# Two mixtures of experts inside a scan kernel: every expert over every token, or each token sorted to its two experts

## The chip, the cores and the metric

The kernel runs on one core of one Trainium2 chip. A core has five engines with queues of their own, each in order: TensorE (PE; its weight loads are listed as PEld), VectorE (DVE), ScalarE (ACT), GpSimd (POOL) and SyncE (SP), which here issues nearly all DMAs. [...] The metric is the device time of one execution in microseconds. Three runs of the kernel before gave 7050.43, 7048.9 and 7061.08 us, with the median 7050.43.

## The reference, cut to what matters

The model has four layers on an input of 4 images of 32 x 32 positions with 256 channels, that is 4 images of 1024 tokens. Layer 0 is a state-space block (512 inner channels, 64 states), layer 1 a convolution block, layer 2 graph attention and a mixture of experts, layer 3 a second state-space block (512 inner channels, 16 states) and a second mixture. The mixtures are the matter here:

```python
# layer 2                                          # layer 3
logits = tokens @ router_w.T                       logits = xf @ gate_w + gate_b
probs = softmax(logits)                            probs = softmax(logits)
rw, re = top_k(probs, 2)                           top2_vals, top2_idx = top_k(probs, 2)
rw = rw / max(rw.sum(-1), 1e-12)
combine = zeros(N, 8).at[rows, re].set(rw)         cw = zeros(N, 8).at[rows, top2_idx].add(top2_vals)
out = tokens
for e in range(8):                                 for each expert:
    h = gelu(tokens @ w1[e] + b1[e])                   h = gelu(xf @ w1 + bb1)
    y = h @ w2[e] + b2[e]                              y = h @ w2 + bb2
    out = out + combine[:, e:e+1] * y                  acc = acc + we[:, None] * y
```

Tokens are the layer-normed activations, and both results are added to the residual. The hidden width is 256 in layer 2 and 512 in layer 3. The weight of six of a token's eight experts is zero, so a token needs two experts only; the reference computes all eight. Everything is f32.

## The kernel before, in words

The work goes image by image. `SCANS` lists eight scans: four of layer 0, named (0, image), and four of layer 3, named (3, image), in the order (0,0) (0,1) (3,0) (0,2) (3,1) (0,3) (3,2) (3,3). A scan is cut into units of 128 partitions by 1024 time steps: 256 units for a layer-0 scan and 64 for a layer-3 scan, 1280 in all. A unit k (function `scans`, line 340 on) does this:

- SP loads the row or rows of step sizes into `dA`, spread over the partitions: two DMAs per unit for layer 0, eight for layer 3. There are five buffers, and the load is written four units ahead.
- ScalarE takes their exponential. PE spreads the inputs into PSUM (`ps_rep`).
- VectorE multiplies `ps_rep` with the row of B and runs the scan itself into `h` (five buffers). POOL multiplies `h` with the row of C.
- PE sums pairs of units over the states into `ps_y`.

All other work is "stages" (`STAGES`): `front` (layer 0 up to the scan), `middle` of an image (the rest of layer 0, layer 1, attention, the layer-2 mixture `moe(2, ...)`, and the front of layer 3) and `last` (the back of layer 3 and `moe(3, ...)`). A stage is a Python generator. `run` (line 503) drives the scans; after every half unit it calls `advance` up to two times, and each call writes down a small piece of the current stage, up to its next `yield`. It stops as long as an estimate of some engine's time, kept by `Metered`, is ahead of VectorE's. So the order of instructions in every engine's queue is fixed when the program is built: pieces of a stage stand between scan units. A stage waits for the scan that it is listed with. Where a scan needs a stage that isn't finished, `need` (line 478) writes the rest of that stage at once, with no scan beside it. After the last unit the rest of the stages is written out, and `last` of image 3 runs alone.

In this order, `middle` of images 0, 1 and 2 and `last` of images 0 and 1 stand wholly under scans. `middle` of image 3 stands partly under scan (3,2) and for its larger part alone, because scan (3,3) needs it. `last` of image 2 stands under scan (3,3) with its second half behind the last unit, and `last` of image 3 stands alone at the end.

`moe` (line 1347) normalizes the tokens into `xn`, transposes them into `xT` (two chunks of 128 channels by 1024 tokens), multiplies with the router into `lg`, and `route` turns that into `cw`, a weight for each token and expert, zero for all but two. The term with b2 is one matmul with `cw` transposed. Then it goes over 16 blocks, each one expert and 512 tokens. PE multiplies with `we1` into `ps_h` (line 298), ScalarE takes the gelu into `h_m` (line 1441), PE multiplies with `we2` into `ps_e` (line 1433), and VectorE adds `ps_e` times the token's weight to the residual `tb` (line 1449). Each expert's weights are loaded once per image, by SP (lines 1350 and 1352), with two buffers. PSUM for the stages is three banks taken in turn (`ps`).

In the profile, instructions recorded through `Metered` all bear line 120; the names of tiles tell them apart.

Of the kernel before, what the change touches and what calls it, by code (L numbers as in the profile page):

```python
# [16 lines left out]
P = 128  # L17
NB = 4
L = 1024
# [5 lines left out]
NEXP = 8  # L25
NEG = -1.0e30
# [29 lines left out]
    (("L2_ffn_b1", 16), ("L3_ffn_b1", 32)),  # L56
# [31 lines left out]
class Metered:  # L88
# [21 lines left out]
    def __getattr__(self, key):  # L110
        got = getattr(self.what, key)
        if self.name is None:
            return Metered(got, self.clock, key) if key in self.COST else got
        cost = self.COST[self.name].get(key)
        if cost is None:
            return got

        def run(*args, **kw):
            self.clock[self.name] += cost(*args, **kw)
            return got(*args, **kw)  # L120

        return run


class Hybrid:
# [352 lines left out]
    def need(self, scan):  # L478

        late = False  # L480
        while ("parts", *scan, DC - 1) not in self.ready:
            if self.advance() is None:
# [6 lines left out]
    def advance(self):  # L489

        if self.stage is None:
# [6 lines left out]
        if cost is None:  # L498
            self.stage = None
            return 0.0  # L500
        return cost

    def run(self):

        self.done, self.ready = set(), set()
        self.todo, self.stage = list(STAGES), None
# [6 lines left out]
        with tc.tile_pool(name="scan", bufs=1) as mp, tc.tile_pool(  # L513
# [6 lines left out]
            for n, _ in enumerate(self.scans(mp, psum)):  # L520
# [3 lines left out]
                for e in clock:  # L524
                    clock[e] = max(clock[e], now - LAG)
                for _ in range(TICKS):
                    if max(clock.values()) > clock["vector"] + LEAD or self.advance() is None:
                        break
            while self.advance() is not None:
# [778 lines left out]
    def prepare_moe(self, st, psum):  # L1308
# [22 lines left out]
        self.gb = self.const.tile([P, NEXP], F32, name="gb")  # L1331
# [4 lines left out]
    def moe(self, which, b, tb):  # L1336

        nc, tc, a = self.nc, self.tc, self.a
        w1, w2, b1, hidden = (
            (a["L2_ffn_w1"], a["L2_ffn_w2"], self.vec["L2_ffn_b1"], 256) if which == 2  # L1340
            else (a["L3_ffn_W1"], a["L3_ffn_W2"], self.vec["L3_ffn_b1"], 512)
        )
        KH = hidden // P
        with tc.tile_pool(name=f"m{which}{b}", bufs=1, side="right") as op:
            xT = op.tile([P, 2, L], F32, name="xTm")
            cw = op.tile([P, TB, NEXP], F32, name="cw")

            def expert_weights(e):
                we1 = op.tile([P, 2, hidden], F32, tag="we1", name="we1", bufs=2)
                nc.sync.dma_start(we1, w1[e].rearrange("(k p) n -> p k n", p=P))  # L1350
                we2 = op.tile([P, KH, C], F32, tag="we2", name="we2", bufs=2)
                nc.sync.dma_start(we2, w2[e].rearrange("(k p) n -> p k n", p=P))
                return we1, we2

            weights = {0: expert_weights(0)}
            with tc.tile_pool(name=f"mg{which}{b}", bufs=1, side="right") as gp:
                xn = gp.tile([P, TB, C], F32, name="xnm")
                yield from self.norm(gp, tb, TB, xn, "lnm")
                yield from self.turned(xn, TB, xT)
# [16 lines left out]
                if which == 2:  # L1376
                    for j in range(0, TB, 2):
                        tj = tb[:, j : j + 2, :]
                        nc.gpsimd.tensor_tensor(tj, tj, xn[:, j : j + 2, :], ALU.add)
                        yield 0.6  # L1380
                yield from self.route(gp, lg, cw, which == 2)
# [12 lines left out]
                got = {}  # L1394
# [15 lines left out]

            hidden_of = {}
            got = {}

            def one(item):
                kind, e, g, i = item
                we1, we2 = weights[e]
                if kind == "h":
                    if i == 0:
                        hidden_of[e, g] = op.tile([P, KH, 512], F32, tag="h", name="h_m", bufs=2)
                        if g == 1 and e + 1 < NEXP:  # L1420
                            weights[e + 1] = expert_weights(e + 1)
                    got[item] = ps = self.ps("ps_h")
                    self.mm(
                        ps, lambda k: we1[:, k, i * P : (i + 1) * P], xT, 2,
                        slice(g * 512, (g + 1) * 512),
                    )
                    return
                h = hidden_of[e, g]
                got[item] = ps = self.ps("ps_e", (P, 2, C))
                for s in range(2):  # L1430
                    m = 2 * i + s
                    for f in range(KH):
                        nc.tensor.matmul(  # L1433
                            ps[:, s, :], lhsT=h[:, f, m * P : (m + 1) * P], rhs=we2[:, f, :],
                            start=(f == 0), stop=(f == KH - 1),
                        )

            def two(item):
                kind, e, g, i = item
                if kind == "h":  # L1440
                    nc.scalar.activation(
                        hidden_of[e, g][:, i, :], got.pop(item), AF.Gelu,
                        bias=b1[:, e * KH + i : e * KH + i + 1],
                    )
                    return
                ps = got.pop(item)
                for s in range(2):
                    m = 4 * g + 2 * i + s
                    nc.vector.scalar_tensor_tensor(  # L1449
                        tb[:, m, :], ps[:, s, :], cw[:, m, e : e + 1], tb[:, m, :],  # L1450
                        ALU.mult, ALU.add,
# [3 lines left out]
            blocks = [(e, g) for e in range(NEXP) for g in range(2)]  # L1455
            for n in range(len(blocks) + 1):
                if n < len(blocks):
# [272 lines left out]
```

## Time and profile before

| What | us |
|---|---|
| median of three runs | 7050.43 |
| the profiled execution | 7061.6 |
| its span, first to last instruction | 7059.5 |
| PE busy in it | 5383.6 |
| VectorE busy in it | 5212.0 |
| POOL busy in it | 3650.0 |
| ScalarE busy in it | 3462.1 |
| VectorE's scan instructions, 1280 | 2924.7 |
| VectorE's products ahead of them, 1280 | 1553.0 |
| POOL's products behind them, 1280 | 3024.2 |

The first scan instruction starts 317.7 us into the span and the last ends at about 6643. From 5743 to 6280 no scan runs, while `middle` of image 3 is finished. The last mixture's experts run from 6830.7 to 7053.1.

A line of the groups by line reads: line, engine, operation, output<-inputs by the program's names, shapes, count | busy us, mean ns of one | idle time of the engine just before them, and what ended it. The DMA share is the busy share of the core's 16 DMA engines.

### The profile page before, as it was taken

Reading aid. Unit: us, or ns where it says so; the run is one execution under the profiler, and the core shown is the slowest. Engines: PE = TensorE matmul, PEld = TensorE weight load, DVE = VectorE, ACT = ScalarE, POOL = GpSimd, SP = SyncE. Lnnn points to the kernel's source line nnn. Section 1 sums busy time; section 2 is a strip of 40 time slices with the busy share of each in tenths; the row PEclk is TensorE's granted clock in tenths of the full one; section 3 lists DMA queues with packets and bytes.
Section 4 is the critical chain, followed back from the end, with each engine's and each line's share of the span. In section 5 each row is a group of like instructions: output and inputs, shape, how many; then the busy total and the mean of one; then the engine's idle time right before and its main releaser. Section 6 shows DMA issues by size and latency. Waiting matters only on the chain. (4 is left out here: it accounts for less than half of the span.)

```text
span 7059.5 us, 66331 instructions
## 1 busy us (share of the span) xinstructions
PE 5383.6 (76%) x20516; PEld 2218.2 (31%) x20516; DVE 5212.0 (74%) x4477; ACT 3462.1 (49%) x4162; POOL 3650.0 (52%) x1801
## 2 busy tenths in 40 slices
PE   7185876578898567879779668898698677957979
PEld 3020221032253022224235332242254322513556
DVE  2787898887898986789889877898899831247511
ACT  3254666244477324447658434577386332244511
POOL 1288677664556754555766554556656520045300
PEclk9585876578888567979879778898698889877989
DMA  2355666654456565446656654456666620135421
GB/s 82 77 139 158 161 178 167 169 143 120 115 143 176 160 172 136 119 116 171 176 151 164 178 144 120 115 143 178 165 168 165 162 70 6 44 107 152 113 63 33
DMA packets 395053, 939.03 MB, mean 133 GB/s; under 512 B 83268, under 2 KB 165776, under 8 KB 393040
## 3 DMA queue, kind: packets, MB, share of 16 engines
q1 hardware_dynamic: 392512, 932.10, 49.0%
q8 instruction: 172, 2.82, 0.2%
q0 software_dynamic: 2128, 2.13, 0.2%
q14 instruction: 241, 1.97, 0.1%
HBM read 844.17 MB, written 93.95 MB: 133 GB/s over the span
## 5 line engine op out<-in xcount | busy, mean ns | idle before, releaser
L120 POOL TENSOR_TENSOR h<-h,rows 128x1024 f32<-128x1024 f32 x1280 | 3024.2, 2365 | 2138.8 <-DVE h L120 1756.0
L120 DVE TENSOR_TENSOR_SCAN h<-dA,ps_rep 128x1024 f32<-128x1024 f32 x1280 | 2924.7, 2285 | 228.0 <-issue 94.6
L120 DVE TENSOR_TENSOR ps_rep<-ps_rep,rows 128x1024 f32<-128x1024 f32 x1280 | 1553.0, 1213 | 338.7 <-PE ps_rep L120 317.0
L120 ACT ACTIVATE dA<-dA,A_L_conv_A_log 128x1024 f32<-128x1024 f32 x1024 | 1152.8, 1145 | 695.2 <-DMA dA<-dt 600.6
L120 PE MATMUL ps_rep<-S,spread_L_conv_A_log 96*128 96x512 bf16 x2048 | 763.2, 463 | 899.6 <-DVE h L120 731.7
L120 PE MATMUL ps_y<-h,collect_L_conv_A_log 128*32 128x512 f32 x4096 | 750.2, 755 | 91.1 <-POOL h L120 91.1
L120 ACT ACT_TABLE_LOAD x494 | 633.8, 1283 | 174.7 <-DMA dA<-dt 115.0
L120 PEld LDWEIGHTS <-spread_L_conv_A_log 96*128 96x128 bf16 x2048 | 164.5, 103 | 1661.3 <-DVE h L120 1213.5
L120 PE MATMUL ps_h<-xTm,we 128*128 128x512 f32 x1280 | 605.2, 609 | 7.6 <-ACT h_m L120 6.6
L120 PE MATMUL ps_e<-we,h_m 128*128 128x256 f32 x2560 | 587.9, 381 | 10.1 <-ACT h_m L120 10.1
L120 ACT ACTIVATE p<-ps_sc 128x512 f32<-128x512 f32 x512 | 277.9, 595 | 587.2 <-PE ps_sc L120 573.8
L120 ACT ACTIVATE dA<-dA,A_L_attn_A_log 128x1024 f32<-128x1024 f32 x256 | 293.6, 1148 | 490.1 <-DMA dA<-dt 456.4
L120 PEld LDWEIGHTS ps_e<-we,h_m 128*128 128x128 f32 x2560 | 481.8, 190 | 140.6 <-issue 46.0
L120 PE MATMUL ps_at<-p,v 128*32 128x512 f32 x1024 | 363.6, 627 | 63.1 <-ACT p L120 55.7
L120 PE MATMUL ps_rep<-S,spread_L_attn_A_log 96*128 96x512 bf16 x512 | 191.4, 464 | 280.8 <-DVE h L120 239.2
L120 ACT ACTIVATE h_m<-ps_h,cols 128x512 f32<-128x512 f32 x320 | 216.5, 687 | 302.2 <-PE ps_h L120 299.3
L120 DVE SCALAR_TENSOR_TENSOR tb<-ps_e,cw,tb 128x256 f32<-128x256 f32 x448 | 192.6, 473 | 200.5 <-PE ps_e L120 200.5
L120 PEld LDWEIGHTS ps_h<-xTm,we 128*128 128x128 f32 x1280 | 242.4, 193 | 288.1 <-issue 236.3
L120 PE MATMUL ps_sc<-qT,kT 32*128 32x512 f32 x1024 | 300.7, 663 | 0.0
L120 PE MATMUL ps_at<-p,ones 128*32 128x512 f32 x1024 | 280.1, 627 | 0.0
L120 DVE RECIPROCAL sums<-sums 128x512 f32<-128x512 f32 x16 | 53.6, 3353 | 253.4 <-ACT sums L120 253.4
L120 PEld LDWEIGHTS ps_y<-h,collect_L_conv_A_log 128*32 128x32 f32 x4096 | 98.8, 119 | 450.4 <-issue 234.3
(406 smaller groups left out, 5703.5 us busy)
## 6 DMA issues: line engine op xcount, KB each, us to landing
dA<-dt SPq DMA_DIRECT2D x2048, 256.0 KB
dA<-dt SPq DMA_DIRECT2D x2048, 64.0 KB
we<-in_L_ffn_W_dram SPq DMA_DIRECT2D x64, 512.0 KB
parts<-parts SPq DMA_DIRECT2D x64, 384.0 KB
S<-parts SPq DMA_DIRECT2D x96, 256.0 KB
dt<-sp_r SPq DMA_DIRECT2D x64, 256.0 KB
y<-yo SPq DMA_DIRECT2D x128, 128.0 KB
y_back<-y SPq DMA_DIRECT2D x64, 256.0 KB
```

What stands on the lines that cost most here:

```text
L120: return got(*args, **kw)
```

## The change

Each token now goes to its two experts only. The 2048 pairs of token and expert of an image are put in order by expert, each expert's run is rounded up to whole tiles of 256, and 15 tiles are computed whatever the routing (2048 / 256 + 8 - 1 is the most that rounding can ask for). In detail:

- `xn` is stored to DRAM as rows (`rows`), one row of 1 KB per token.
- `route` keeps the two choices apart (`hot`), and the new `sort` works out, with small matmuls and comparisons: how many tokens each expert has, how many tiles that makes, the place of each pair in the order (`place`), the expert of each tile (`expert`), the token of each place (`token`), each pair's weight (`share`), and the b1 column of each tile (`bias`).
- For each tile, SP reads the expert's number into a register and loads that expert's weights from the address it gives (again for every tile, four and five buffers, two tiles ahead). POOL gathers the tile's 256 rows with two indirect DMAs of 128 rows. PE transposes them, and then runs the two matmuls with the gelu between as before, on 256 rows. ScalarE copies the result out of PSUM, and SP stores it in DRAM (`done`).
- At the end, POOL gathers each token's two results with 16 indirect DMAs (`y_b`, four buffers), and VectorE adds them times `share` to `tb`, one tile two steps after its gather.
- `Hold` is a `yield` that keeps stages from advancing for some half units of the scan, unless they are forced: `advance` compares the half unit with `until`.
- The addition of `xn` to the layer-2 residual moves behind the b2 term; the b1 vectors move out of the packed vectors into tiles of their own; `prepare_moe` makes a few constant tables.

The diff, cut to its core:

```diff
+SLOTS = 256
+TILES = 2 * L // SLOTS + NEXP - 1
...
-    def advance(self):
-
+    def advance(self, forced=False):
+
+        if self.half < self.until and not forced:
+            return None
...
+        if isinstance(cost, Hold):
+            self.until = self.half + cost
...
-            xT = op.tile([P, 2, L], F32, name="xTm")
-            cw = op.tile([P, TB, NEXP], F32, name="cw")
-
-            def expert_weights(e):
-                we1 = op.tile([P, 2, hidden], F32, tag="we1", name="we1", bufs=2)
-                nc.sync.dma_start(we1, w1[e].rearrange("(k p) n -> p k n", p=P))
-                we2 = op.tile([P, KH, C], F32, tag="we2", name="we2", bufs=2)
-                nc.sync.dma_start(we2, w2[e].rearrange("(k p) n -> p k n", p=P))
-                return we1, we2
...
+            def room(n):
+                xs[n] = [op.tile([P, C], F32, tag=f"x{s}", name=f"x_t{s}", bufs=3) for s in range(NS)]
+
+            def gather(n, s):
+                if n < TILES:
+                    x = xs[n][s]
+                    nc.gpsimd.indirect_dma_start(
+                        out=x, out_offset=None, in_=rows,
+                        in_offset=bass.IndirectOffsetOnAxis(
+                            ap=token[:, NS * n + s : NS * n + s + 1], axis=0
+                        ),
+                        bounds_check=L - 1, oob_is_err=False,
+                    )
...
+            def weights(n):
+                if n < TILES:
+                    e = nc.sync.value_load(expert[:, n : n + 1], min_val=0, max_val=NEXP - 1)
+                    for w, to in zip((w1, w2), we[n]):
+                        nc.sync.dma_start(to, w[bass.ds(e, 1)].rearrange("o p k n -> (o p) k n"))
...
+                nc.sync.dma_start(rows.rearrange("(p j) c -> p j c", j=TB), xn)
...
-                yield from self.route(gp, lg, cw, which == 2)
+                yield from self.route(gp, lg, cw, hot, both, which == 2)
+                yield from self.sort(gp, which, hot, both, cw, place, share, token, expert, bias)
+                for n in range(2):
+                    weights(n)
+                    gather(n, 0)
+                    gather(n, 1)
+                    yield 1.0
+                gather(2, 1)
...
+                if kind == "x":
+                    if n + 2 < TILES:
+                        weight_room(n + 2)
+                    weights(n + 2)
+                    ps = got[item] = self.ps("ps_xt", (P, 2, NS, P))
+                    for k in range(2):
+                        for s in range(NS):
+                            nc.tensor.transpose(
+                                ps[:, k, s, :], xs[n][s][:, k * P : (k + 1) * P], self.ident
+                            )
...
+                    gather(n + 2, 0)
...
+                    yo = op.tile([P, NS, C], F32, tag="yt", name="y_t", bufs=2)
+                    nc.scalar.copy(yo, got.pop(("o", n)))
+                    nc.sync.dma_start(
+                        done[n * SLOTS : (n + 1) * SLOTS, :].rearrange("(s p) c -> p s c", p=P), yo
                     )
...
-                for s in range(2):
-                    m = 4 * g + 2 * i + s
-                    nc.vector.scalar_tensor_tensor(
-                        tb[:, m, :], ps[:, s, :], cw[:, m, e : e + 1], tb[:, m, :],
-                        ALU.mult, ALU.add,
-                    )
...
+            yield from self.pipe(items, one, two, cost=1.7)
+            yield Hold(4)
+
+            def back(q):
+                y = got[q] = op.tile([P, C], F32, tag="yb", name="y_b", bufs=4)
+                nc.gpsimd.indirect_dma_start(
+                    out=y, out_offset=None, in_=done,
+                    in_offset=bass.IndirectOffsetOnAxis(ap=place[:, q : q + 1], axis=0),
+                    bounds_check=TILES * SLOTS - 1, oob_is_err=False,
+                )
...
+            def add(q):
+                i, j = divmod(q, TB)
+                nc.vector.scalar_tensor_tensor(
+                    tb[:, j, :], got.pop(q), share[:, i, j : j + 1], tb[:, j, :],
+                    ALU.mult, ALU.add,
+                )
+
+            yield from self.pipe(range(2 * TB), back, wait, add, cost=1.0)
+
+    def sort(self, gp, which, hot, both, cw, place, share, token, expert, bias):
...
+        nc.vector.tensor_tensor(
+            reach, placef.unsqueeze(2).to_broadcast([P, 2 * TB, blocks + 1]),
+            self.block.unsqueeze(1).to_broadcast([P, 2 * TB, blocks + 1]), ALU.is_ge,
+        )
...
+        at = gp.tile([P, 2 * TB, P], BF16, name="at")
+        nc.vector.tensor_tensor(
+            at, low.unsqueeze(2).to_broadcast([P, 2 * TB, P]),
+            self.count.unsqueeze(1).to_broadcast([P, 2 * TB, P]), ALU.is_equal,
+        )
+        yield 2.2
+
+        own = gp.tile([P, 2 * TB, blocks], F32, name="own")
+        nc.gpsimd.tensor_tensor(own, reach[:, :, :blocks], reach[:, :, 1:], ALU.subtract)
+        of = gp.tile([P, 2, 2 * TB, blocks], BF16, name="of")
+        nc.vector.tensor_scalar(of[:, 0], own, self.part8, None, ALU.mult)
+        nc.gpsimd.tensor_tensor(
+            of[:, 1].rearrange("p (i j) k -> p i j k", i=2),
+            own.rearrange("p (i j) k -> p i j k", i=2),
+            self.count[:, :TB].unsqueeze(1).unsqueeze(3).to_broadcast([P, 2, TB, blocks]), ALU.mult,
+        )
+        yield Hold(2)
+        ps = self.ps("ps_tk")
+        for q in range(2 * TB):
+            for i in range(2):
+                nc.tensor.matmul(
+                    ps[:, :blocks], lhsT=at[:, q, :], rhs=of[:, i, q, :],
+                    start=(q == 0 and i == 0), stop=(q == 2 * TB - 1 and i == 1),
+                )
...
+        nc.vector.tensor_copy(token, ps[:, :blocks])
```

## The prediction

> **What bounds the kernel now.** I read the page first, then the busy times by stretch, the chain of waits, the groups by line and SP's own waits. The page says that no engine is busy throughout, so the bound has to be read stage by stage.
>
> ```profile
> span 7059.5 us, 66331 instructions
> PE 5383.6 (76%) x20516; PEld 2218.2 (31%) x20516; DVE 5212.0 (74%) x4477; ACT 3462.1 (49%) x4162; POOL 3650.0 (52%) x1801
> L120 DVE TENSOR_TENSOR_SCAN h<-dA,ps_rep 128x1024 f32<-128x1024 f32 x1280 | 2924.7, 2285 | 228.0 <-issue 94.6
> L120 DVE TENSOR_TENSOR ps_rep<-ps_rep,rows 128x1024 f32<-128x1024 f32 x1280 | 1553.0, 1213 | 338.7 <-PE ps_rep L120 317.0
> L120 DVE SCALAR_TENSOR_TENSOR tb<-ps_e,cw,tb 128x256 f32<-128x256 f32 x448 | 192.6, 473 | 200.5 <-PE ps_e L120 200.5
> ```
>
> A scan unit costs VectorE 2.285 + 1.213 = 3.50 us, and 1280 of them are 4478 us of the span. The other stages are threaded between the units, except where no scan can run. By stretch:
>
> ```profile
> 3670.60:3961.90 291.30, 280.91 (x1168) 151.26 (x1166) 278.96 (x213) 237.07 (x223) 176.32 (x75) 1.00 0.61 164
> 4634.00:4770.80 136.80, 133.57 (x551) 73.61 (x549) 132.64 (x130) 115.35 (x108) 75.49 (x32) 1.00 0.57 149
> 5743.00:6279.60 536.60, 435.51 (x1612) 185.89 (x1611) 82.96 (x189) 180.21 (x298) 61.98 (x50) 0.91 0.09 31
> 6499.00:6641.00 142.00, 126.52 (x506) 66.37 (x504) 122.94 (x92) 107.06 (x103) 76.24 (x33) 0.98 0.58 151
> 6641.00:6758.00 117.00, 115.38 (x421) 77.20 (x420) 17.64 (x37) 22.80 (x33) 3.82 (x2) 1.00 0.10 30
> 6831.00:7053.00 222.00, 222.00 (x768) 146.16 (x767) 27.63 (x63) 43.97 (x64) 0.00 (x0) 0.99 0.09 29
> ```
>
> The columns are stretch, length, then PE, PEld, VectorE, ScalarE and POOL busy, PE clock, DMA share, GB/s. Rows one and two are the experts of a layer-3 and a layer-2 mixture under a scan: VectorE is 96% busy, so a unit waits for VectorE. Row three has one layer-2 mixture (6031 to 6144) without a scan, rows five and six are layer-3 mixtures after the last scan: PE alone. The chain shows one block of 512 tokens and one expert there, 6.87 + 6.91 = 13.78 us, 16 of them 220 us:
>
> ```profile
> 7004.84 6.87 PE ps_h L298 x16
> 7011.71 6.91 PE ps_e L1433 x32
> ```
>
> In row four the scan is (3,3) with eight row loads a unit. SP waited there almost only for a DMA's semaphore, never long for a free buffer, so SP's issue sets the pace:
>
> ```profile
> SPq L394 <- DMA we<-in_L_ffn_W_dram: 6.1, 4, 2.4
> SPq L394 <- DVE h L120: 0.7, 2, 0.4
> ```
>
> **What the Trainium skill says.** "SBUF — State Buffer", Who interferes with whom: a VectorE instruction with two SBUF inputs contends with a GpSimd instruction that reads SBUF. The trace agrees: the split's subtraction takes 691 ns when free and 1546 in the median, beside POOL's 2.37 us products. Sums read from PSUM (the 473 ns row) show no such spread.
>
> ```profile
> L120 DVE TENSOR_TENSOR sp_x<-sp_l,parts x56: 691/1546/2171, 532.5 to 6277.5; 128x512 f32<-128x512 f32 x56
> L120 POOL DMA_INDIRECT mask_dram<-zero,where x64: 993/1001/1316, 322.7 to 599.2; - x64
> ```
>
> "DMA: Bandwidth & Descriptors", SWDGE vs HWDGE vs iDMA: DMAs of POOL and of SP end on the same 16 engines, which take turns between queues. No run here has both heavy. The same page, Latency and other measured facts, puts a load of a register from memory at some 600 ns; the attention's own on SP shows 281 ns and 0.6 us with the checks behind it.
>
> **The change, part by part.**
>
> *PE work.* Before, each layer-3 mixture is 16 x 13.78 = 220 us and each layer-2 one 110 (half the hidden width; its 113 us agree). After, a 256-row tile is half a block, 6.9 us (3.45 in layer 2), plus four transposes of 0.31 us (16 took 5.03 us at 6804.7) = 1.26. So 15 x 8.18 = 123 us and 15 x 4.70 = 71 us. Less 97 and 39.
>
> *Added chain.* The sort is some 20 small VectorE steps (0.17 to 0.28 each, like the router's), three long ones (496 elements 0.65, 464 elements 0.65, 2048 elements 2.4, scaled from 1.2 ns an element), two POOL products of 480 elements (1.2 each), 32 small matmuls (estimate 3.5): about 15 us on end. The bias term behind it (9 us, 6822 to 6831) hides the first gathers (1.0 us on POOL, 2.1 to 3.2 us to landing) and first weights. At the end come the last store (ScalarE copy 0.6, SP 0.45, landing about 2.2), 16 gathers back at 1.0 us each on POOL and one landing and sum (4): 23.5 us.
>
> *Where PE is alone.* Last mixture: from 6821.8 comes 15 + 9 + 2 (fill) + 123 + 23.5 = end at 6994, against 7053.6: **-59 us**. Mixture of row five: before, 113 us remain after the last scan. In the changed program's order 3 tiles' transposes, 4 tiles' first and 5.5 tiles' second matmuls stand behind the last unit: 3 x 1.26 + 9.5 x 3.45 = 37, plus 23.5 = 60: **-53**. Layer-2 mixture of row three: 6022 + 15 + 9 + 71 + 23.5 = 6141 against 6144: **0** (within 12).
>
> *SP in row four.* Per tile a register load with checks 0.6, two loads at a computed address 2 x 0.55, a store 0.5 = 2.2 us. 11 tiles fall under scan (3,3): 24, less 2.8 for the loads of before: **+22**, since every row load of the scan is queued behind on SP. Under the other scans (two loads a unit, 1.1 us of 3.5) SP has room.
>
> *Under the scans: six mixtures.* VectorE loses 64 x 0.473 = 30.3 us and some 4 us of waits for the first expert. It gains the sort, 8 us, the 16 sums, 16 x 0.475 = 7.6, and waits: the first of a run of two-SBUF-input steps behind POOL's product waits 0.7 to 2.0 us (five to eight of them, 8 us); the sort's steps wait for PE twice (1.7 each, as the router's first copy does) and for POOL's product (2.6); the sums come two ticks behind their gather, less than 1.0 + 3.2 us, about 4. Sum 34.5 against 34.5: **0**. POOL: 46 x 1.01 + 2.4 = 49 us more a mixture; in 69 units its products are 163 us, so 212 of some 265: it fits. Behind a POOL wait stand the scan's products, five buffers deep.
>
> *DMA under the scans.* Row six moves 6.4 MB (222 us at 29 GB/s) in 20 us of 16-engine time: 3.1 us/MB. Row one is 178 us of it for 76 units; less 26 for 8.4 MB of weights, 2.0 us a unit. A layer-3 tile is now 1.05 MB of weights, 0.26 gathered, 0.26 stored, 4.9 us per 3.4 units: 1.44. Together **3.44 of 3.50 us**. Layer 2: 3.25 per 2.2 units, 1.48: 3.5. The row loads run four units ahead, so I let a unit stretch by 0.2 us over 33 or 51 units: **+8** a mixture, +48. Bounds: 0 (the share reached 1.0 in short bursts) to +25, if the queues reach 85% only (4.1 us a unit).
>
> Sum: -59 - 53 + 22 + 48 = **-42**. Against the profiled span of 7059.5 us (2.1 us less than that execution's time, 7061.6) that is 7017.5; on the median, 7050.4, it is **7008 us**.
>
> **Rivals.**
> - *DMA becomes the bound under the scans* (other side). Place: the gather phases of the six mixtures; price 0.6 us a unit, 25 us a mixture, 102 more than above: 7110. It decides from 15 to 16 us a mixture (unit 3.86 us), where the 90 us saved without scans are spent. For it: 3.44 of 3.5 us demanded, and weights stand before row loads in SP's one queue. Against: VectorE ran 3.5 us a unit at share 0.65 (2338 to 2555).
> - *VectorE's 30 us come free*: sums and sort cost 15.5 us without waits and DMA is hidden, -19 a mixture: -114 - 90, about 6850 to 6900. Against: the 1546 ns row.
> - *Gathering costs POOL twice as much* (2 us for rows of 1 KB; the trace has only 4-byte elements): POOL then needs 260 of 265 us a mixture, units wait for their product buffers, and each tail of gathers grows by 16: +30 a mixture, +48 in the tails: about 7230.
> - That it doesn't do what it says is excluded by the program's order: 15 tiles of transposes and matmuls stand in each mixture.
>
> **How the numbers follow.** Chances: forecast 0.45 (own range 6955 to 7045), DMA rival 0.35, free VectorE 0.12, dear gathers 0.08. 0.2% is 14 us, about what a measurement of this kernel can tell from no change. Of the forecast 0.38 lies below 7036 and 0.07 within; of the DMA rival 0.02 is within. Faster 0.38 + 0.12 = 0.50, same 0.09, slower 0.41. The range cuts half of the free case and the dear one: 6910 to 7150.
>
> **What would show it.** Right: the last mixture near 170 us with PE at 8.2 us a tile; the stretch after the last scan down by half; the layer-2 mixture without a scan unchanged; scan (3,3) longer by 20 us with SP without gaps; under scans, about the same time for the same units, DMA share above 0.85. Wrong: ScalarE waiting for row loads by tens of us a mixture (DMA), POOL above 90% (gathers), VectorE idle before sums or the token list (the waits are longer than I set), or a tile without a scan above 8.2 us because weights or rows come late.

## The result, and the profile after

The changed kernel takes 7138.55 us in the median of four runs (7117.31 to 7146.82), where the kernel before took 7050.0 beside it: a ratio of 1.0117, interval 1.0093 to 1.0142. So it is 1.2% slower. In a later comparison the ratio was 1.0119 (1.0102 to 1.0136). The forecast was 7008; its own range ended at 7045, the range over all its cases at 7150.

The engines are less busy than before, PE by 468 us, and the span is longer. These are lines of the page of the changed kernel: the span, the busy times and three groups (busy and mean, then idle time before and what ended it).

```profile
span 7115.6 us, 67338 instructions
PE 4915.4 (69%) x19731; PEld 1998.0 (28%) x19731; DVE 5193.8 (73%) x4260; ACT 3266.2 (46%) x4222; POOL 4048.1 (57%) x2186
L123 ACT ACTIVATE dA<-dA,A_L_conv_A_log 128x1024 f32<-128x1024 f32 x1024 | 1158.5, 1146 | 968.0 <-DMA dA<-dt 880.9
L123 POOL DMA_INDIRECT x_t<-rows,token x210 | 215.3, 1025 | 58.2 <-issue 31.7
L123 DVE SCALAR_TENSOR_TENSOR tb<-y_b,share,tb 128x256 f32<-128x256 f32 x112 | 89.0, 813 | 182.2 <-DMA y_b<-done,place 182.2
```

The same group of exponentials, in the page of the kernel before:

```profile
L120 ACT ACTIVATE dA<-dA,A_L_conv_A_log 128x1024 f32<-128x1024 f32 x1024 | 1152.8, 1145 | 695.2 <-DMA dA<-dt 600.6
```

ScalarE waits 280 us longer for the scan's row loads. Of VectorE's 182 us for gathered rows, 137 stand where no scan runs, in stages where it waited 184 us for `ps_e` before; under the scans it is 45 us, where 17 for `ps_e` stood. A sum that took 473 ns takes 813 in the mean: 484 without a scan, 922 to 975 in the five mixtures under scans. A gather of 128 rows costs POOL 1.03 us, as forecast. Now by stretch (stretch, length, busy PE, PEld, VectorE, ScalarE, POOL, PE clock, DMA share, GB/s): the tiles of a layer-3 and of a layer-2 mixture under a scan, layer 2 of image 3 alone, scan (3,3), the rest of layer 3 of image 2, the last mixture's tiles and its gathers back.

```profile
3756.40:3956.90 200.50, 171.59 (x838) 111.04 (x836) 171.82 (x101) 162.32 (x195) 143.18 (x76) 0.96 0.92 238
4733.00:4871.00 138.00, 103.62 (x502) 61.28 (x501) 115.14 (x70) 104.25 (x125) 113.21 (x67) 0.91 0.91 235
5888.00:6414.70 526.70, 388.39 (x1584) 168.09 (x1583) 70.52 (x161) 187.39 (x327) 112.54 (x98) 0.87 0.19 59
6640.20:6820.80 180.60, 133.97 (x580) 87.88 (x581) 114.06 (x67) 112.91 (x137) 100.29 (x55) 0.86 0.82 201
6823.00:6895.00 72.00, 33.88 (x159) 27.74 (x157) 7.82 (x17) 11.43 (x25) 20.19 (x20) 0.75 0.38 116
6969.00:7082.00 113.00, 112.53 (x535) 98.56 (x535) 0.00 (x0) 41.55 (x89) 23.09 (x23) 0.97 0.58 164
7082.00:7110.00 28.00, 0.18 (x1) 0.00 (x0) 7.68 (x16) 0.58 (x1) 16.28 (x16) 0.55 0.28 85
```

Row one is where VectorE was 96% busy; it is 86% busy now, and the DMA engines are at 0.92. Where PE is alone the change does what it says: 113 us for 15 tiles. The chain of the tail shows a tile, 3.46 + 3.45 us and 0.44 of transposes, and the drain behind the last one:

```profile
7020.84 3.46 PE ps_h L1522 x16
7024.29 3.45 PE ps_e L1530 x16
...
7082.26 0.59 ACT y_t L1551
7082.87 2.12 DMA done<-y_t
7085.99 5.49 DMA y_b<-done,place x2
```

The starts of the scan instructions in the two traces give the account by stretch (a number of a unit is the number of its scan instruction). Up to unit 1203 the scans took 5425.5 us and take 5575.9 (+150); layer 2 of image 3, alone between units 1203 and 1204, 536.4 and 526.5 (-10); units 1204 to 1279, with scan (3,3), 361.7 and 406.1 (+44); what follows, 418.2 and 294.8 (-123). The second profile of the changed kernel, 7130.1 us long and nearer its median, has 5592.8, 526.3, 404.9 and 293.1; the comparisons below are with that one. The tails came about as forecast (-112 and 0). The scans cost 195 to 210 us, where +70 was forecast (48 for the DMAs, 22 for SP). The experiments ask what these are. PE's granted clock fell too, from 1.00 to 0.96 in row one, but PE is busy 171.6 of 200.5 us there; whether a lower clock adds to the loss was not tried by itself.

One suspect was not in the forecast. SP's own waits among the tiles of row one (total us, times, longest):

```profile
SPq L1552 <- ACT y_t L123: 81.5, 14, 8.0
SPq L401 <- DVE h L123: 11.0, 14, 2.3
SPq L401 <- DMA we<-in_L_ffn_W_dram: 8.4, 5, 3.5
```

Line 1552 is the store of a finished tile. SP stands 81.5 of 200.5 us at it, waiting for ScalarE's copy, with the row loads (line 401) queued behind. So beside "the bytes fill the DMA engines" (D) there is "SP's one queue is held up" (Q).

How a late row load reaches VectorE is read from three waits of the same stretch together:

```profile
ACT dA L123 <- DMA dA<-dt: 27.6, 10, 8.8
PE ps_h L123 <- ACT y_t L123: 19.2, 10, 2.9
DVE ps_rep L123 <- PE ps_rep L123: 15.2, 11, 4.4
```

ScalarE waits for the row at its exponential, with a tile's copy `y_t` behind it; PE waits for that copy to free a bank, with the scan's `ps_rep` behind; and VectorE waits for `ps_rep`.

### The profile page after: what moved, and what is told of

It is laid out like the page before. It is cut to its first block, busy times and chain, and to the rows that moved or that the text cites. A ratio compares the mean times of both kernels' runs of the same rounds, so it can differ in the third digit from the quotient of the medians.

```text
span 7115.6 us, 67338 instructions
## 1 busy us (share of the span) xinstructions
PE 4915.4 (69%) x19731; PEld 1998.0 (28%) x19731; DVE 5193.8 (73%) x4260; ACT 3266.2 (46%) x4222; POOL 4048.1 (57%) x2186
## 5 line engine op out<-in xcount | busy, mean ns | idle before, releaser
L123 PE MATMUL ps_rep<-S,spread_L_conv_A_log 96*128 96x512 bf16 x2048 | 794.7, 480 | 1152.0 <-DVE h L123 962.7
L123 PE MATMUL ps_y<-h,collect_L_conv_A_log 128*32 128x512 f32 x4096 | 802.0, 793 | 88.9 <-POOL h L123 88.7
L123 PE MATMUL ps_h<-x_tt,we 128*128 128x256 f32 x1200 | 330.3, 425 | 126.9 <-ACT y_t L123 77.0
L123 PE MATMUL ps_e<-we,h_m 128*128 128x256 f32 x1200 | 294.8, 387 | 11.2 <-ACT y_t L123 6.5
L123 PEld LDWEIGHTS ps_h<-x_tt,we 128*128 128x128 f32 x1200 | 241.6, 209 | 214.2 <-ACT y_t L123 94.3
L123 PEld LDWEIGHTS ps_e<-we,h_m 128*128 128x128 f32 x1200 | 228.2, 193 | 83.8 <-issue 24.4
L123 POOL DMA_INDIRECT x_t<-rows,token x210 | 215.3, 1025 | 58.2 <-issue 31.7
L123 DVE SCALAR_TENSOR_TENSOR tb<-y_b,share,tb 128x256 f32<-128x256 f32 x112 | 89.0, 813 | 182.2 <-DMA y_b<-done,place 182.2
```

## The experiments

Ratios are to the kernel before on the same chip; 0.001 is 7 us. Four comparisons gave the kernel before 7049, 7057, 7046 and 7051 us, so ratios are compared, and a gain against the changed kernel is the difference of two ratios. Each ratio has an interval of 8 to 17 us to either side; medians of one comparison differ from such a gain by up to 7 us.

**Sorted only where no scan runs.** The dense mixture of before is kept beside the new one, and each mixture picks one:

```diff
+SORTED = [(2, 3), (3, 3)]
     def moe(self, which, b, tb):
+        if (which, b) in SORTED:
+            yield from self.moe_sorted(which, b, tb)
+        else:
+            yield from self.moe_dense(which, b, tb)
```

> The sorted form only where no scan runs beside it: layer 2 of image 3 and layer 3 of image 3; the other six mixtures are the dense ones of before. Theory (all the loss sits under the scans, the tails are gains as forecast): the layer-2 mixture brings about -10 us and the last one about -72 us (232 to 160 us after its routing, by the two traces), 7050 - 82 = about 6968 us (6955 to 6985), and every unit of the scans up to 1203 takes what it took before, within 3 us in sum. Rival (part of the loss is a cost that the whole program bears, such as a lower granted clock or later loads after a sorted mixture): 7000 us or more.

Measured: 6968.3 us, ratio 0.9885 (0.9868 to 0.9901). The scans up to unit 1203 took 5415.4 us, 10 less than before and not within the 3 expected; in the two other runs that change nothing up to there they took 5418.5 and 5430.6, so 15 us is what this number scatters by. Busy times of units 746 to 821, the experts of layer 3 of image 0, in this run:

```profile
3653.60:3946.50 292.90, 285.76 (x1188) 156.20 (x1192) 279.03 (x213) 243.05 (x228) 177.77 (x76) 1.00 0.62 162
```

The same units before took 292.6 us. The gain of the tails is real and stands alone, and the whole loss belongs to the mixtures under scans. What follows unit 1279 took 342.6 us instead of 418.2: the last mixture brings 76, for 59 forecast.

**The same, with layer 3 of image 2 sorted too** (`(3, 2)` added to the list).

> As the run before, and layer 3 of image 2 sorted too, which begins under the last scan (3,3) and ends after it. By the two traces of before and after, the scan's last 51 units took 238 us and took 282 us (+44) and the rest after the scan lost about 51 of its 123 us there. Theory (both sizes hold where this mixture is changed alone): within 10 us of the run before, about 6960 to 6975 us, unit time of the last 33 units 5.4 to 5.5 us. Forecast on record (+22 under the scan, -53 after it): 31 us below the run before, about 6937 us. Rival (the slow scan units are left over from earlier sorted mixtures): last 33 units at 4.5 us or less and about 6925 us.

Measured: 6961.55 us, ratio 0.9876 (0.9860 to 0.9893), faster than both kernels and the lowest of the versions that leave nothing out, though not clear of the run before. The last 33 units took 180.3 us (142.4 in the kernel before), and 294.7 us follow (342.6 in the run before). So this mixture gives about as much as it takes, and the slowing of scan (3,3) is its own. The forecast's 31 us of gain are refuted.

**Static weights.**

```diff
-                    for w, to in zip((w1, w2), we[n]):
-                        nc.sync.dma_start(to, w[bass.ds(e, 1)].rearrange("o p k n -> (o p) k n"))
+                    for w, to in zip((w1, w2), row[n]):
+                        nc.sync.dma_start(to, w[bass.ds(e, 1), 0, 0])
```

> The changed kernel, but the two weight loads of each tile fetch one row each (2 KB and 1 KB) into a buffer that nobody reads, and all tiles multiply by one set of weights that is loaded once in each mixture: it leaves out the experts' own weights, 15 MB of loads in a layer-3 mixture and half of that in a layer-2 one; the number of loads, register loads and their places in the queues stay. After-kernel 7138 us. Theory D (under the scans the DMA engines' bytes are the bound, busy share 0.91): 60 to 90 us faster, 7050 to 7080 us, gather units of the layer-3 mixtures at 3.4 to 3.7 us instead of 4.12 and 4.24. Theory Q (SyncE's queue is held up by the store of a finished tile, which waits for ScalarE's copy, with the scan's dA loads queued behind it; bytes don't matter): within 20 us of the changed kernel, units at 4.0 us or more. Forecast's own cost of the bytes (+8 per mixture): 40 to 50 us faster.

Measured: 7012.25 us, ratio 0.9943 (0.9927 to 0.9960), 124 us below the changed kernel. The tiles of layer 3 of image 0, and the last 33 units:

```profile
3735.20:3916.90 181.70, 164.56 (x838) 107.97 (x836) 170.65 (x101) 163.25 (x194) 143.14 (x76) 0.99 0.75 192
6564.70:6718.50 153.80, 122.10 (x570) 79.41 (x573) 113.95 (x66) 110.16 (x134) 101.21 (x55) 0.91 0.58 150
```

A unit among the tiles falls to 3.63 us (181.7 by 50), close to VectorE's own 3.50. D holds, and more is lost to the bytes than either number said. In row two SP issues as many DMAs as in the changed kernel (one of the small loads takes it 0.25 us instead of 0.37), and the units under scan (3,3) are 25 us shorter than in its second profile. SP's waits show where most of that lies, first in the changed kernel (6640.2 to 6820.8), then here:

```profile
SPq L401 <- DMA we<-in_L_ffn_W_dram: 18.3, 13, 2.4
SPq L401 <- DMA dA<-dt: 3.4, 9, 0.9
SPq L401 <- DMA S<-parts: 3.0, 3, 1.4
```

```profile
SPq L401 <- DMA S<-parts: 2.6, 3, 1.0
SPq L401 <- DMA dA<-dt: 1.4, 3, 0.6
SPq L401 <- DVE h L123: 0.7, 2, 0.5
```

Before a row load (line 401) SP waits until a weight load has landed, and with small weight loads it doesn't. It hardly waits for a free buffer (`h`) in either run, so SP's queue sets the pace there.

**Late store.**

```diff
+            def store(item):
+                kind, n, i = item
+                if kind == "o" and i == NS - 1:
+                    nc.sync.dma_start(done[...], got.pop(("y", n)))
-            yield from self.pipe(items, one, two, cost=1.7)
+            yield from self.pipe(items, one, two, idle, idle, store, cost=1.7)
```

> The changed kernel, with the store of each finished tile issued three steps of its pipeline later (about 8 us), so that the copy it waits for is done when SyncE comes to it; nothing is left out. Theory Q (SyncE's queue is held up by that store): the wait of 8.0 us mean goes, gather units fall to 3.5 to 3.8 us, 60 to 90 us faster than the changed kernel, 7050 to 7080 us. Theory D (bytes are the bound): the wait on the store goes but the dA loads land as late as before, within 15 us of the changed kernel, 7125 to 7150 us.

Measured: 7102.45 us, ratio 1.0066 (1.0043 to 1.0089), 37 us below the changed kernel: neither Q's 60 nor D's 15. (`y_t` has three buffers here instead of two.) The tiles of layer 3 of image 0:

```profile
3754.40:3956.50 202.10, 173.30 (x838) 112.06 (x836) 171.55 (x101) 164.22 (x195) 143.06 (x76) 0.96 0.96 238
```

With SP free of that wait the engines are at 0.96, and a unit still takes 4.04 us. Q was part of it, and D is what lies below.

**Weights on ScalarE's queue**, in the changed kernel and in the version with three sorted mixtures:

```diff
-                    e = nc.sync.value_load(expert[:, n : n + 1], min_val=0, max_val=NEXP - 1)
+                    e = nc.scalar.value_load(expert[:, n : n + 1], min_val=0, max_val=NEXP - 1)
-                        nc.sync.dma_start(to, w[bass.ds(e, 1)].rearrange("o p k n -> (o p) k n"))
+                        nc.scalar.dma_start(to, w[bass.ds(e, 1)].rearrange("o p k n -> (o p) k n"))
```

> The changed kernel, with each tile's register load and its two weight loads issued by ScalarE's queue instead of SyncE's: the same bytes, and SyncE's queue keeps the scan's dA loads and the stores. The run with static weights was 126 us faster than the changed kernel (7138 us), so the weights cost about that; this tells how. Theory F (first in, first out: in SyncE's queue a dA load waits behind 1 MB of weights that it could overtake in a queue of its own): 50 us or more faster than the changed kernel, 7090 us or less, dA waits of ScalarE gone. Theory B (capacity: the engines are full, whatever queue the bytes come by): 7115 to 7150 us, DMA share in the layer-3 gather units still above 0.9 and 4.0 us a unit or more.

> Sorted only for layer 2 of image 3 and layer 3 of images 2 and 3 (6962 us with all loads on SyncE), with the weights on ScalarE's queue as in the run before. Under the scan (3,3) the DMA engines' share was 0.82 only, so there is room. Theory F (the dA loads of 64 KB wait in line behind the weights): the scan's last 33 units fall from 180 to 150 to 160 us as with static weights, total 6930 to 6942 us. Theory B (capacity): the units stay at 175 us or more, 6955 to 6970 us. The forecast's own mechanism (SyncE needs 2.2 us of issuing for each tile, 1.2 of it for the weights): half of its 22 us goes, 6950 us.

Measured: 7083.01 us, ratio 1.0042 (1.0027 to 1.0056), and 6977.58 us, ratio 0.9889 (0.9872 to 0.9905). The last 33 units of the second:

```profile
6491.00:6686.60 195.60, 143.22 (x574) 91.14 (x573) 113.97 (x66) 112.83 (x135) 102.17 (x56) 0.81 0.71 181
```

The first meets F by its total (54 us less than the changed kernel) and B among the tiles of layer 3 of image 0:

```profile
3748.10:3945.10 197.00, 174.82 (x838) 112.60 (x836) 171.80 (x101) 163.61 (x194) 143.27 (x76) 0.93 0.94 241
```

That is a share of 0.94 and 3.94 us a unit. The last pair below parts the two. In the second, the units under scan (3,3) take 195.6 us, not 150 to 160, with 1.2 us a tile taken off SP. That refutes F there. The traces show why it is 15 us more and not less: SP's largest wait in these units (total, times, longest), first with the weights on SP's queue and then on ScalarE's, is

```profile
SPq L403 <- DMA we<-in_L_ffn_W_dram: 18.1, 13, 2.5
```

```profile
SPq L403 <- DMA we<-in_L_ffn_W_dram: 51.4, 21, 4.8
```

The 180.4 us less all of SP's waits leave 151.5 for its issuing, the 195.6 us leave 133.8. So the issuing went as the forecast's mechanism says, and more than that came back as waits for weight loads that ScalarE had issued. Why a row load waits for their landing, and longer so, the traces don't show.

**Static weights and late store together.**

> Static weights (the experts' own weights left out as in that run) and the store of a finished tile three steps later. With static weights alone: 7012 us, and SyncE still waited 25 us for the copy in the layer-3 gather units. If the store's wait costs by itself: 25 to 40 us less, as late store alone brought (-36), so about 6975 to 6987 us. If it costs only where the engines are full (the loads are late already and every delay is passed on): 7005 to 7015 us, within 8 us of static weights alone.

Measured: 7014.12 us, ratio 0.9940 (0.9924 to 0.9957), the same as static weights alone. So what was left of the store's wait costs nothing once the weights' bytes are gone. It was a shorter wait, though: 25 us among these tiles with static weights, 81.5 in the changed kernel.

**Late sums.**

```diff
-                y = got[q] = op.tile([P, C], F32, tag="yb", name="y_b", bufs=4)
+                y = got[q] = op.tile([P, C], F32, tag="yb", name="y_b", bufs=8)
-            yield from self.pipe(range(2 * TB), back, wait, add, cost=1.0)
+            yield from self.pipe(range(2 * TB), back, wait, wait, wait, add, cost=1.0)
```

> The changed kernel, with the sums three steps behind their gathers instead of two and eight row buffers instead of four; nothing left out. In the trace VectorE waits 8 to 10 us in each mixture under the scans for gathered rows, and the sums take 1006 ns beside the scan where 470 ns stand alone. If the waits are for gathers issued too late: they go, 25 to 45 us faster (7095 to 7113 us). If the rows come late because POOL issues them late or the engines are full: within 10 us of the changed kernel, 7128 to 7148 us, and the wait stands at another row.

Measured: 7098.12 us, ratio 1.0059 (1.0042 to 1.0076), 42 us below. The traces account for less. VectorE's waits for gathered rows up to unit 1203, in the second profile of the changed kernel and here:

```profile
DVE tb L123 <- DMA y_b<-done,place: 41.9, 26, 4.7
```

```profile
DVE tb L123 <- DMA y_b<-done,place: 24.2, 10, 3.8
```

So 18 us of waits were for gathers issued too late, and 24 us stayed. The rest of the 42 isn't traced: the profiled run is the slowest of its four, 19 us below the changed kernel's.

**The changed kernel again, without its sort, and without sort and weights.** For the second and third, `sort` is not called and the lists are constants:

```diff
-                yield from self.sort(gp, which, hot, both, cw, place, share, token, expert, bias)
+            place, share, token, expert = self.lists
+            bias = self.nobias[:, :KH, :]
```

> The changed kernel once more, unedited, beside the next three, since its first profile (7117 us) was its fastest run and late store and late sums came out 36 and 41 us below its median (7138 us) while their profiles differ from its own by 5 us. If the first median stands: ratio 1.0117 to the kernel before, 7130 to 7150 us. If it was high: 7100 to 7120 us, ratio 1.008, and then late store and late sums brought next to nothing.

> The changed kernel without the sort: the lists of places, tokens, experts and shares are constants made once at the start, so the 15 tiles run over fixed rows with fixed experts; the sort's work on VectorE, TensorE and POOL and the biases are left out, all gathers, weights, tiles and sums stay. By the phases of the trace the sort takes 20 and 16 us more than the units of before in the two layer-3 mixtures, about 8 us in each of the three layer-2 mixtures, 15 us in each of the two that run alone and 6 us under the scan (3,3): 96 us less than the changed kernel, about 7040 us. Forecast on record (18 us under a scan: 8 of work, half of the 8 us of waits of two-SBUF-input instructions, 6 for TensorE and POOL; 15 us alone): 6 x 18 + 2 x 15 = 138 us less, about 7000 us. Rival (the sort stands mostly beside waits that come anyway): under 50 us less, above 7088 us.

> Both left out: the sort as in the run before, and the experts' own weights as with static weights. If the two costs are independent: the 126 us of the weights and what the run before finds (96 expected), about 6916 us, with the scan units of the gather phase at 3.6 to 3.75 us. If the weights only cost because the sort leaves the scan's buffers empty at the start of the tiles: their saving shrinks to under 90 us, above 6950 us.

Measured: 7130.51 us, ratio 1.0119 (1.0102 to 1.0136), the first median stands; 7010.59 us, ratio 0.9951 (0.9934 to 0.9968), 118 us less, between the 96 of the trace and the forecast's 138; and 6909.0 us, ratio 0.9804 (0.9787 to 0.9820), 222 us less. The two costs come within 20 us of adding up. Of the sort's saving 79 us lie before unit 1203, 7 in units 1204 to 1279, and 29 where no scan runs.

Even without sort and weights the units up to 1203 take 5443.2 us, 18 more than before (the number scatters by 15). So a third cost is left, which takes what the sums taken off VectorE should have brought: 48 a mixture at 0.473 us, 114 us over the five.

**Both delays**, store and sums together (two buffers of `y_t`, six of `y_b`).

> The changed kernel with both delays: the store of a tile three steps later and the sums three steps behind their gathers (six row buffers). Nothing left out. If the two gains seen (36 and 41 us) are real and stand in different places: 7060 to 7075 us, still not below the kernel before. If they share a cause or were chance: 7090 to 7120 us.

Measured: 7072.65 us, ratio 1.0046 (1.0029 to 1.0062), 51 us below the changed kernel (58 by the medians of this comparison), less than 37 and 42 together. Tiles and sums of layer 3 of image 0:

```profile
3737.20:3935.00 197.80, 174.54 (x842) 113.79 (x841) 172.02 (x103) 160.47 (x192) 142.86 (x76) 0.95 0.96 245
3935.00:3985.90 50.90, 18.08 (x58) 2.12 (x58) 45.30 (x35) 11.49 (x10) 38.93 (x26) 0.53 0.58 152
```

Row two is units 804 to 813, which hold the sums. In the second profile of the changed kernel they took 5 us more:

```profile
3965.10:4021.00 55.90, 17.22 (x54) 2.19 (x58) 44.95 (x34) 11.12 (x11) 37.81 (x26) 0.50 0.52 143
```

VectorE's wait for gathered rows in them, first in the changed kernel and then with both delays, fell by the same 5 us (total, times, longest):

```profile
DVE tb L123 <- DMA y_b<-done,place: 10.1, 6, 4.4
```

```profile
DVE tb L123 <- DMA y_b<-done,place: 5.0, 2, 3.1
```

**Order or capacity.** Both delays, and the weights on ScalarE's queue except in layer 3 of image 2; and both delays with static weights.

> The changed kernel with both delays (7073 us, ratio 1.0046) and the weights on ScalarE's queue, except in layer 3 of image 2, where that queue cost 14 us. Nothing left out. If order in SyncE's queue still costs: another 30 to 50 us off, ratio 0.998 to 1.000, gather units at 3.7 us. If capacity sets the rest: within 15 us of the run with both delays, ratio 1.003 to 1.006, units at 3.85 us or more and the DMA share at 0.95.

> Both delays and static weights (the experts' own weights left out). If capacity is the larger part of the 118 to 126 us: 70 us or more below the run with both delays, about 7000 us or less, ratio 0.994 or less. If the two delays had already taken most of the weights' cost: within 40 us of it, about 7040 us.

Measured: 7072.72 us, ratio 1.0029 (1.0018 to 1.0040), not clear of both delays alone; and 6977.56 us, ratio 0.9901 (0.9884 to 0.9917), 102 us below them. Tiles of layer 3 of image 0, in the first and in the second:

```profile
3751.80:3950.20 198.40, 172.63 (x843) 112.78 (x841) 171.76 (x103) 160.05 (x191) 142.58 (x75) 0.95 0.95 238
```

```profile
3720.70:3903.30 182.60, 168.42 (x843) 110.36 (x841) 171.38 (x102) 159.93 (x191) 142.40 (x75) 0.98 0.73 187
```

A queue of their own brings the weights nothing clear of noise once SP isn't held up. The Trainium skill says why ("DMA: Bandwidth & Descriptors", Issuing engines are not separate DMA queues): all issuers' DMAs end on the same 16 engines, and a second issuer saves issuing time alone. These two runs agree. So of the 124 us of the weights about 100 remain with the store's wait and the late gathers out of the way, and these are the bytes themselves. The 22 us between are within the two intervals and aren't shown to be the order of SP's queue.

## Why the prediction was wrong

The mechanism of the first rival, the DMA engines as the bound under the scans, is the larger part of what happened, and it had the sign (7110 for a chance of 0.35). That its sum came near 7138 is in part luck: it put 150 us on the DMAs of six mixtures, where the weights' bytes cost 117 to 124, and nothing on VectorE, where 75 came; the tails brought 21 us more than it had. By the forecast's own steps:

*Where PE is alone: right.* The layer-3 mixtures at the end brought -123 us for -112, the layer-2 one -10 for 0, within the 12 given. A tile took 7.35 us for 8.18: four transposes cost 0.44 us together and not 1.26. The drain took 27.8 us (7082.3 to 7110.1) for 23.5: the 16 gathers back start from 7086.0 to 7106.5, 1.37 us apart and not 1.0. The first experiment measured these gains by themselves.

*Gathers on POOL: right.* 1.03 and 1.01 us each, and POOL has room.

*DMA under the scans: the first step that failed.* It set the weights at 3.1 us of 16-engine time a megabyte, from a stretch where little else moved, and got 3.44 us of demand for each 3.50 us unit. Beside the scan a megabyte costs more: with both delays the tiles held the engines for 197.8 x 0.96 = 190 us and 48.5 MB, with static weights for 181.7 x 0.75 = 136 us and 34.9 MB; 3.9 us a megabyte in both, and for the difference. A tile's 1.57 MB are then 6.1 us per 3.4 units, 1.8 us a unit instead of 1.44, and with the scan's 2.0 us 3.8: above the 3.50 that VectorE needs. From the profile of before most of this could be had: its row one shows 0.61 x 291.3 us for 164 x 291.3 kB, 3.7 us a megabyte. With that price a unit demands 3.7 us, and 3.87 at the share of 0.96 that the engines reached; both delays gave 197.8 / 50 = 3.96. The forecast used that row for the scan's part only. Forecast: +8 a mixture. Measured, by static weights against the changed kernel: 92 us over the five mixtures up to unit 1203 and 25 in units 1204 to 1279.

*Under the scans, VectorE: "34.5 against 34.5" failed too*, and by more: for the five mixtures the forecast had 40 us for the DMAs and 0 here. (The terms it lists add up to 34.3 and 33.6.) With static weights the units up to 1203 still take 75 us more than before, where the step said 0. For layer 3 of image 0 the traces give the excess over 3.50 us a unit, in us:

| | router, b2 | sort | tiles or experts | sums | behind | total |
|---|---|---|---|---|---|---|
| before | 28.2 | - | 30.1 | - | 18.9 | 77.2 |
| changed, second profile | 21.4 | 24.5 | 33.8 | 24.5 | 18.4 | 122.7 |
| static weights | 22.0 | 24.5 | 6.6 | 24.5 | 17.4 | 95.0 |
| both delays | 23.3 | 26.9 | 22.8 | 19.4 | 20.1 | 112.5 |
| both delays, static | 29.2 | 29.8 | 7.6 | 19.4 | 17.3 | 103.3 |

(Units 729 to 746, 746 to 754, 754 to 804, 804 to 813 and 813 to 835; before, 746 to 821 for the experts and 821 to 835 behind them.) The sort was sized well: 18 us a mixture in the forecast, 16 over the five when it is left out, 24.5 in its own units here with 7 less around them. The sums were not: 7.6 of work, 4 of waits and half of the 8 for instructions with two SBUF inputs make 15.6, and 24.5 came. The experts' work gave back 30.1, not 34.5, and the tiles cost 6.6 where their bytes are left out and nothing was set. Together 8.9 + 4.4 + 6.6 = 20 us; this mixture's 17.9 (static weights against before) agrees, and the other layer-3 mixture's 19 to 23, by the unit where it is taken to begin. Of the sums' 24.5, 10.1 are the waits shown above. Their work, in seven mixtures of which five stand under scans, and in the last mixture (line 1580), as minimum, median and maximum in ns:

```profile
L123 DVE SCALAR_TENSOR_TENSOR tb<-y_b,share,tb x112: 455/484/2571, 2143.0 to 6883.2; 128x256 f32<-128x256 f32 x112
...
L1580 DVE SCALAR_TENSOR_TENSOR tb<-y_b,share,tb x16: 483/484/485, 7088.9 to 7109.6; 128x256 f32<-128x256 f32 x16
```

Without POOL's products beside them all 16 take 484 ns; under the scan, in layer 3 of image 0, they average 974, eleven of them at 0.46 to 0.49 us and five at 1.7 to 2.6. That agrees with the Trainium skill ("SBUF — State Buffer", Who interferes with whom), which the forecast used, but it spread its 8 us over the sort and the sums where the sums alone lost 8 (with both delays the 16 took 15.7 us in those units, at 0.48 they are 7.7). The delay of the sums confirms the waits; that the ports are the rest was not tried by itself. In the layer-2 mixtures VectorE also waits 5.3 us for POOL's `tb` before the layer norm (units 330 to 367 took 174.9 us and take 180.5, and twice more so). The norm stands half a unit earlier there; its cause was only argued.

*SP under scan (3,3): right mechanism, with a term put at nothing.* +22 was forecast for SP's issuing (24 less 2.8 is 21), and the stretch from unit 1204 lost 43. For the last 33 units, in us (issuing is the length less SP's waits):

| | length | waits for landings | other waits | issuing |
|---|---|---|---|---|
| before | 142.4 | 7.5 | 1.4 | 133.5 |
| changed, second profile | 179.1 | 20.5 | 3.9 | 154.7 |
| static weights | 153.8 | 4.3 | 0.9 | 148.6 |
| three sorted | 180.4 | 25.4 | 3.5 | 151.5 |
| three sorted, ScalarE's queue | 195.6 | 61.0 | 0.8 | 133.8 |

Issuing grew by 18 to 21 us, as forecast. The term left out is SP's waiting for DMAs to land, 13 to 18 us more with the weights and less than before with static weights. So the bytes cost time here at a mean share of 0.82, because SP, which sets the pace, stands still until weight loads have landed. The forecast had seen such waits before (6.1 us) and didn't let them grow.

## What to carry to other kernels

Removed arithmetic pays only where its engine is the bound: here the same edit brought 133 us in the stages that PE held alone and lost about 200 under scans that VectorE, the DMA engines and SP's queue held. Before trading operations for loads, price the new bytes at what a megabyte costs in the stage where they will run, and compare the sum with the time of the stage's bound; a stretch with idle engines prices them too low. And where an edit pays in some stages only, make it in these: three of eight mixtures sorted gave 0.9876 of the time before, two of eight about the same (0.9885).

## What was not expected of the hardware

The 16 DMA engines were full (share 0.96 to 0.97) at 238 to 248 GB/s with loads of rows, weights and gathered rows mixed. The Trainium skill gives about 358 GB/s as the HBM limit of one core, and 425 as measured for one transfer of 16 MB ("DMA: Bandwidth & Descriptors", Where 436 GB/s comes from); among the tiles the mean stays far below it, single slices of 5 us reach 340, and the measured number decides for this mix. Half of the bytes among the tiles are row loads (102 of 256 KB each, 27 of 49 MB), which spread a row of 4 KB over 64 partitions and are counted once for each partition.

A wait in SP's queue (81.5 of 200.5 us among the tiles of one mixture) cost 37 us over the whole kernel while the DMA engines were full. With the weights' bytes gone it was 25 us and cost nothing: SP then had slack, 62 us of waits for free buffers among the same tiles instead of 11 to 19.

SP's row loads also waited for weight loads of another queue to land: 51.4 us in 21 waits under scan (3,3) when ScalarE issued them, 18.1 in 13 when SP did. Moving a DMA to another engine's queue took its issuing away but not the wait for it.
